# Attention and feed-forward layer on one core: the softmax sums' reciprocals taken on one row per head, by way of DRAM

## The chip, the cores and the metric

One Trainium2 chip, one core of it. The metric is the device time of one execution in microseconds (us), as the median of several runs.

## What is computed

```python
x  = L0_attn_x                                  # (2, 1024, 512), fp32
Q  = (x @ Wq.T + bq)  ->  32 heads of 16;  K, V: 8 heads of 16, each used by 4 query heads
Q, K = rope(Q, K)
w  = softmax(Q @ K.T / sqrt(16))                # per batch and head, 1024 x 1024
x  = layernorm(x + (w @ V) @ Wo.T + bo)
h  = silu((x @ gate_w.T) * gate_s) * ((x @ up_w.T) * up_s)     # 1408 wide
x  = layernorm(x + (h @ down_w.T) * down_s)
```

## The kernel before, in words

**Units, quarters, turns.** The attention is cut into 32 units (`UNITS`, line 37): batch, half of the sequence (512 queries), and one of the 8 K/V heads `g` with its 4 query heads. Eight units of one batch and half make a quarter (0 to 3). Each unit has 8 steps of 128 keys. The main loop (line 684) takes two steps at a time; this document calls one pass of it a *turn*, c = 0 to 127. Unit u has turns 4u to 4u+3 for its exponentials.

**Inside a turn** TensorE follows an order written out by hand (lines 669 to 676): `F`, one piece of other work (fill); `A`, products of Q and K for the row maxima, 12 steps ahead (`max_pass`, line 326), each read by a VectorE maximum (line 342); `B`, the same products again with the maximum subtracted (`exp_pass`, line 363), read by a ScalarE exponential (line 379); and the slots `V0` and `V1`, where the weights of two steps before are multiplied with V (`av`, line 383). Stretches between two turns are measured from V0 to V0. The PSUM banks that hold what TensorE has made and the others have not read are few: four for A and fill, three for B.

**The sums.** The V operand `va` holds a one beside each of its columns (line 137), so a unit's result `pv` has 128 rows: for each of 4 heads 16 pairs of a numerator and the sum of the weights. All 16 sum rows of a head are the same. V1 of turn 4u+4 ends unit u and calls `unit_out` (line 400): ScalarE copies `pv` to `o` (line 406), and SP moves the even rows into `num` and the odd rows into `den` (lines 413 and 414), two transfers of 64 rows of 2 KB. Two units with an even and the next odd g share one `num` and one `den` of 128 rows: a pair. After the odd one, VectorE takes the reciprocal of `den` in four pieces of 128x128 (line 419) and multiplies `num` by it (line 424). There are 16 pairs, the last two units' pair among them.

**When.** Work that is to wait goes by `after(n, f)` (line 192), run in the V slot n steps later (two steps are one turn). `early` (line 189) runs at the start of a given turn, ahead of its F. Before the change a pair's reciprocals stand at the start of turns c+2 and c+3 and the product at c+4, where c is the turn in which the pair's second unit ended; at the end of a quarter (g = 7) the reciprocals stand at the next V0 and V1 and the product at the V0 after these, because three turns after the quarter's end its projection (`project`, line 470) reads `num`.

**Fill.** In turns 0 to 20 it is the projections to Q, K and V (`qk_block`, line 236). VectorE and ScalarE also round 33 pieces of the feed-forward weights in turns 2 to 18 (`piece_round`, line 167), two a turn, and SP stores the rounded pieces (`wsd<-sr`) and loads those of two turns later (`sw`). From turn 35 on the fill is the projection and feed-forward of the quarter before (`quarter`, line 609). Turns in between, and those at a quarter's end, have none.

**SP.** All transfers are issued by SP, in the order of the program, and an instruction that waits holds up all behind it: Q and K stores (`qT`, `kT`), weight pieces, `num` and `den`, the maxima through DRAM (`md`, `mt` in `max_rows`, line 344), the loads of a unit's Q and K (`KS`, `QH`, `QL` in `prep`, line 311), weights (`wt`, `wd_sb`), residual rows (`xq`, `xs`) and results. `max_rows` runs at the end of turns 4k+1, one of them right behind every unit's end.

Of the kernel before, what the change touches and what calls it, by code (L numbers as in the profile page):

```python
# [7 lines left out]
F32 = mybir.dt.float32  # L8
# [3 lines left out]
ALU = mybir.AluOpType  # L12
# [4 lines left out]
P = 128  # L17
B, T, D = 2, 1024, 512
HQ, HKV, HD = 32, 8, 16
G = HQ // HKV  # L20
E = 32
# [7 lines left out]
HALF = 512  # L29
NH = T // HALF  # L30
# [16 lines left out]
def attn_ffn_kernel(tc, x, wqkv, bqkv, wo, bo, rope, wg, wu, wd, gs, us, ds, out):  # L47
    nc = tc.nc

    def pool(name, bufs=1, **kw):  # L50
        return tc.alloc_tile_pool(name=name, bufs=bufs, **kw)
# [3 lines left out]
    dram2 = pool("dram2", 2, space=DRAM)  # L55
    ap1 = pool("ap1")
    ap2 = pool("ap2", 2)
# [96 lines left out]
    def piece_load(i):  # L154
        if i >= PIECES:
            return
        SW[i] = sp4.tile([P, D], F32, tag="sw", name="sw")
        if i < 2 * NF:
            f, up = divmod(i, 2)
            nc.sync.dma_start(  # L160
                out=SW[i].rearrange("p (c n) -> p c n", n=P),
                in_=(wu if up else wg)[:, :, f * P : (f + 1) * P],
            )
        else:
            nc.sync.dma_start(out=SW[i], in_=wd[:, i - 2 * NF, :])

    def piece_round(i):
        w = SW.pop(i)
        SR[i] = sp4.tile([P, D], F32R, tag="sr", name="sr")
        nc.scalar.copy(SR[i], w)  # L170

        nc.vector.scalar_tensor_tensor(
            low, w.bitcast(I32), LOW, low, ALU.bitwise_and, ALU.bitwise_or
        )

    def piece_store(i):
        nc.sync.dma_start(out=wsd[i], in_=SR.pop(i).bitcast(F32))
# [8 lines left out]
        after(4, lambda: nc.vector.tensor_reduce(flag, flr, AX.X, ALU.max))  # L186

    later = {}
    early = {}
    now = [0]  # L190

    def after(n, f):
        later.setdefault(now[0] + n, []).append(f)
# [132 lines left out]
    def max_pass(n, j, i):  # L326
        u, s = divmod(n, US)
        t, half = divmod(s, NH)
        if u not in MX:
            MX[u] = ap2.tile([P, TH, G, NH], F32, tag="mx", name="mx")  # L330
        r = slice(j * E, (j + 1) * E)
        if i == 0:
            PA[n, j] = ps_a[0].tile([P, HALF], F32, tag="pa", name="pa")
        nc.tensor.matmul(  # L334
            PA[n, j],
            (QH, QL)[i][u][r, t * P : (t + 1) * P],
            KS[u][r, half * HALF : (half + 1) * HALF],
            start=i == 0,
            stop=i == 1,
        )  # L340
        if i == 1:
            nc.vector.tensor_reduce(MX[u][:, t, j, half : half + 1], PA.pop((n, j)), AX.X, ALU.max)  # L342
# [36 lines left out]
            nc.scalar.activation(prob[:, j, :], PB.pop((n, j)), AF.Exp, scale=SCALE)  # L379

    PV, PVN, NUM = {}, {}, {}

    def av(n, prob):
        u, kc = divmod(n, US)
        b, qh, g = UNITS[u]
        done = PVN[u] = PVN.get(u, -1) + 1
        if done == 0:
            PV[u] = ps_v.tile([P, HALF], F32, tag="pv", name="pv")
        for j in range(G):
            nc.tensor.matmul(  # L390
                PV[u][j * E : (j + 1) * E, :],
                vas[b][:, kc, g, :, :].rearrange("p d o -> p (d o)"),
                prob[:, j, :],
                start=done == 0,
                stop=done == US - 1,
            )
        if done == US - 1:
            unit_out(u)

    def unit_out(u):  # L400


        b, qh, g = UNITS[u]
        q = u // HKV
        o = ap1.tile([P, HALF], F32, tag="o", name="o")
        nc.scalar.copy(o, PV.pop(u))  # L406
        if g % 2 == 0:
            NUM[q, g // 2] = ap4.tile([P, HALF], F32, tag="num", name="num")
            NUM["den"] = ap1.tile([P, HALF], F32, tag="den", name="den")
        num, den = NUM[q, g // 2], NUM["den"]  # L410
        r0 = (g % 2) * G * HD
        rows = slice(r0, r0 + G * HD)
        nc.sync.dma_start(out=num[rows, :], in_=o[0:P:2, :])
        nc.sync.dma_start(out=den[rows, :], in_=o[1:P:2, :])
        if g % 2:
            c = now[0] // 2
            for k in range(TH):
                ns = slice(k * P, (k + 1) * P)
                f = lambda ns=ns: nc.vector.reciprocal(den[:, ns], den[:, ns])  # L419
                if g == HKV - 1:  # L420
                    after(k // 2 + 1, f)
                else:
                    early.setdefault(c + 2 + k // 2, []).append(f)
            f = lambda: nc.vector.tensor_tensor(num, num, den, ALU.mult)
            if g == HKV - 1:
                after(3, f)
            else:
                early.setdefault(c + 4, []).append(f)


    XQ, FP = {}, {}
    DONE = set()
    LASTQ = B * NH - 1

    def load_residual(q, t):
        b, qh = divmod(q, NH)
# [33 lines left out]
    def project(q, t):  # L470
        py = bank("py")
        for c in range(NC):
# [6 lines left out]
            )  # L479
        if q == LASTQ:  # L480
            row = XQ[q, t]
# [26 lines left out]
    def hidden(q, f, up):  # L508
# [13 lines left out]
        if not up:  # L522
# [15 lines left out]
        pus = FP["tmp"].tile(  # L538
            [P, HALF], F32, tag="pus" if q == LASTQ else "th", name="pus"
        )  # L540
        nc.scalar.mul(pus, p, ust[:, f : f + 1])  # L541

        def rest():
            nc.gpsimd.tensor_tensor(z, pus, z, ALU.mult)  # L544
            if q == LASTQ:
                nc.scalar.copy(hi, z)
# [7 lines left out]
    def down(q, t, f0=0, f1=NF):  # L554
# [14 lines left out]
        ys = fp1.tile([P, D], F32, tag="ys", name="ys")  # L569
        if q == LASTQ:  # L570
            nc.vector.tensor_tensor(ys, pd, dsb, ALU.mult)
# [8 lines left out]
        def store():  # L580
# [4 lines left out]
            for i in range(TH):  # L585
                if (q + 1, i) not in XQ and q < LASTQ and (q + 1, i) not in DONE:
                    if i <= t + (q + 1 == LASTQ):
                        DONE.add((q + 1, i))
# [89 lines left out]
    def v_hook(n):  # L678
        now[0] = n
        for f in later.pop(n, ()):  # L680
            f()

    before = None
    for c in range(STEPS // 2):
        probs = {}

        pieces = [i for i in (2 * c - 4, 2 * c - 3) if 0 <= i < PIECES]
        for i in pieces:
            piece_round(i)
        if pieces:  # L690
            after(1, lambda ps=pieces: [(piece_store(i), piece_load(i + 4)) for i in ps])
        for f in early.pop(c, ()):
            f()
        alone = 2 * c + LEAD >= STEPS
        has_fill = bool(fill) and fill[0][0] <= c
        if c >= (STEPS - QS) // 2:
            has_fill = has_fill and len(fill) > 2
        for s in NO_A if alone else WITH_FILL if has_fill else NO_FILL:
            if s == "F":
                if has_fill:  # L700
                    fill.pop(0)[1]()

                    while c < (STEPS - QS) // 2 and (rest := len(fill) % PHASES) and QS // 2 - 1 - c % (QS // 2) < rest < DOWNS:
                        fill.pop(0)[1]()
                continue
            n = 2 * c + int(s[-1])
            if s[0] == "V":
                v_hook(n)
                if before is not None:
                    av(n - 2, before[n - 2])  # L710
                continue
            j, i = int(s[1]), "abc".index(s[2])
            if s[0] == "A":
                max_pass(n + LEAD, j, i)
                continue
            if i == 2 and n not in probs:
                probs[n] = ap3.tile([P, G, HALF], F32, tag="prob", name="prob")
            exp_pass(n, j, i, probs.get(n), alone)
        before = probs
        u, s = divmod(2 * c + 1, US)  # L720
        if s == US - 1 and u + 3 < len(UNITS):
            prep(u + 3)
        if (2 * c + 1 + LEAD) % US == US - 1 and not alone:
            max_rows((2 * c + 1 + LEAD) // US)
        if c == QS // 2 - 10:
            low_flag()
        if c == QS // 2 - 6:
            sp4.release()
            qp4.release()
            qp2.release()  # L730
            qp1.release()
            fp1 = pool("fp1", side="right")
            fp2 = pool("fp2", 2, side="right")
            fp5 = pool("fp5", 5, side="right")
            wd_sb = fp1.tile([P, NF, D], F32R, name="wd_sb")
            nc.sync.dma_start(
                out=wd_sb.bitcast(F32), in_=wsd[2 * NF : PIECES].rearrange("f p n -> p f n")
            )
            FP["tmp"] = fp1
            ask_weights(RING - 1)  # L740
            for t in range(TH):
                load_residual(0, t)
            for q in range(B * NH - 1):
                fill.extend(quarter(q))
# [15 lines left out]
    n = 2 * STEPS  # L760
# [137 lines left out]
```

## Time and profile before

| | |
|---|---|
| runs of the kernel | 1229.11, 1231.25, 1236.65 us, median 1231.25 |
| profiled execution | 1231.15 us |
| its span, first to last instruction | 1229.3 us |
| mean granted TensorE clock | 0.973 of full speed |
| busy: TensorE / VectorE / ScalarE / GpSimd | 1174.0 / 875.3 / 704.4 / 353.2 us |
| transfers by SP | 125.30 MB, 32.0% of the 16 engines' span |

Lines of the profile: `L342 DVE TENSOR_REDUCE mx<-pa 128x1 f32<-128x512 f32` is line 342 of the kernel on VectorE, writing tile mx from tile pa. PE is TensorE, PEld its weight loads, DVE VectorE, ACT ScalarE, POOL GpSimd, SPq the queue of SP. The windows view gives, for a stretch of time, its length, then the busy time of each engine with the number of its instructions, the granted TensorE clock, the busy share of the DMA engines and GB/s. In a timeline a row starts with its start and length in us; in brackets stands the idle time before it and what ended it. In the view of waits, the three numbers are us in total, times, and the longest one.

### The profile page before, as it was taken

How to read it: one execution, taken by the hardware profiler on the slowest of the kernel's cores; microseconds unless marked ns; L12 is line 12 of the kernel's file. 1: busy time of each engine (PE TensorE's matmuls, PEld its weight loads, DVE VectorE, ACT ScalarE, POOL GpSimd, SP SyncE). 2: the span in 40 equal slices, each digit the busy share in tenths (PEclk: the TensorE clock that was granted, in tenths of full speed). 3: DMA queues.
4: the chain of work that ended last, by engine and by line, in shares of the span. 5: the costliest groups of instructions: out<-in, count | busy, mean ns of one | idle time of the engine just before them, and what ended most of it. 6: DMA issues, size and time to landing. Idle time of an engine off the chain costs nothing.

```text
span 1229.3 us, 22709 instructions
## 1 busy us (share of the span) xinstructions
PE 1174.0 (96%) x8784; PEld 611.6 (50%) x8784; DVE 875.3 (71%) x1492; ACT 704.4 (57%) x1300; POOL 353.2 (29%) x340
## 2 busy tenths in 40 slices
PE   8799999999999999999999999999899999999996
PEld 5354445444444544545544544556444454554585
DVE  3579898878877787876677878784758878732434
ACT  2016767656655677675445777774536776774251
POOL 3127262540103122223522222225412222225431
PEclk9769999999989999999999999999999999999899
DMA  5357777442612222221212222221312222111230
GB/s 161 103 190 241 257 243 253 147 162 55 206 45 61 80 79 79 80 82 67 88 33 82 79 79 79 79 79 56 110 36 94 82 79 79 50 49 53 94 121 37
DMA packets 82291, 126.80 MB, mean 103 GB/s; under 512 B 15873, under 2 KB 29442, under 8 KB 82050
## 3 DMA queue, kind: packets, MB, share of 16 engines
q1 hardware_dynamic: 82178, 125.30, 32.0%
q8 instruction: 71, 1.16, 0.4%
q14 instruction: 42, 0.34, 0.1%
HBM read 80.43 MB, written 36.44 MB: 95 GB/s over the span
## 4 chain that ended last, share of the span: by engine, by line
PE 73%; DVE 17%; DMA 3%; POOL 3%; issue 2%; ACT 1%; SPq 0%; POOLq 0%; DVEq 0%; ACTq 0%
PE pb L371 16%; PE pv L390 16%; PE pg L514 13%; PE pa L334 12%; DVE mx L342 9%; PE pq L242 5%; PE pd L560 5%; PE py L473 4%; DVE den L419 3%; DVE st L458 1%; POOL xq L577 1%; POOL ys L576 1%; ACT prob L379 1%; DMA fl<-red 1%; PE pv L293 1%
## 5 line engine op out<-in xcount | busy, mean ns | idle before, releaser
L342 DVE TENSOR_REDUCE mx<-pa 128x1 f32<-128x512 f32 x1024 | 644.5, 682 | 183.7 <-PE pa L334 179.6
L379 ACT ACTIVATE prob<-pb 128x512 f32<-128x512 f32 x1024 | 545.7, 599 | 268.9 <-PE pb L371 253.5
L334 PE MATMUL pa<-KS,QH 32*128 32x512 f32 x1024 | 364.9, 469 | 33.6 <-DVE mx L342 15.0
L334 PE MATMUL pa<-KS,QL 32*128 32x512 f32 x1024 | 350.5, 433 | 0.1
L371 PE MATMUL pb<-QH,KS 32*128 32x512 f32 x1024 | 318.1, 475 | 1.0 <-ACT prob L379 1.0
L390 PE MATMUL pv<-prob,va 128*32 128x512 f32 x2048 | 277.1, 613 | 0.0
L371 PE MATMUL pb<-QL,KS 32*128 32x512 f32 x1024 | 273.5, 421 | 0.0
L371 PE MATMUL pb<-mt,ones 32*128 32x512 f32 x1024 | 256.7, 397 | 0.0
L334 PEld LDWEIGHTS pa<-KS,QH 32*128 32x128 f32 x1024 | 152.8, 187 | 157.9 <-DVE mx L342 131.9
L544 POOL TENSOR_TENSOR z<-pus,z 128x512 f32<-128x512 f32 x44 | 56.3, 1279 | 449.8 <-ACT pus L541 422.6
L371 PEld LDWEIGHTS pb<-QH,KS 32*128 32x128 f32 x1024 | 134.3, 183 | 83.1 <-issue 50.5
L371 PEld LDWEIGHTS pb<-QL,KS 32*128 32x128 f32 x1024 | 127.6, 184 | 86.1 <-issue 85.5
L334 PEld LDWEIGHTS pa<-KS,QL 32*128 32x128 f32 x1024 | 162.9, 189 | 5.7 <-DMA QL<-qT 0.9
L371 PEld LDWEIGHTS pb<-mt,ones 32*128 32x128 f32 x1024 | 140.4, 185 | 25.3 <-issue 17.3
L514 PE MATMUL pg<-x1h,wt 128*128 128x512 f32 x352 | 146.3, 416 | 0.7 <-ACT x1h L503 0.7
L514 PE MATMUL pg<-x1l,wt 128*128 128x512 f32 x352 | 139.4, 396 | 0.3 <-DVE x1l L504 0.3
L390 PEld LDWEIGHTS pv<-prob,va 128*32 128x32 f32 x2048 | 40.9, 108 | 94.5 <-issue 83.3
L514 PEld LDWEIGHTS pg<-x1h,wt 128*128 128x128 f32 x352 | 67.0, 190 | 38.1 <-issue 22.7
L242 PE MATMUL pq<-xT,wqkv_sb 128*128 128x512 f32 x160 | 77.7, 632 | 0.0
L514 PEld LDWEIGHTS pg<-x1l,wt 128*128 128x128 f32 x352 | 67.1, 191 | 13.1 <-DVE x1l L504 0.8
L560 PE MATMUL pd<-wd_sb,hh 128*128 128x512 f32 x176 | 69.9, 397 | 0.7 <-ACT o L406 0.7
L560 PE MATMUL pd<-wd_sb,hl 128*128 128x512 f32 x176 | 68.6, 390 | 0.0
(80 smaller groups left out, 978.5 us busy)
## 6 DMA issues: line engine op xcount, KB each, us to landing
wt<-wsd SPq DMA_DIRECT2D x88, 256.0 KB
KS<-kT SPq DMA_DIRECT2D x128, 128.0 KB
wsd<-sr SPq DMA_DIRECT2D x33, 256.0 KB
qT<-hi SPq DMA_DIRECT2D x16, 512.0 KB
qT<-lo SPq DMA_DIRECT2D x16, 512.0 KB
QH<-qT SPq DMA_DIRECT2D x32, 256.0 KB
QL<-qT SPq DMA_DIRECT2D x32, 256.0 KB
xs<-in_x_dram SPq DMA_DIRECT2D x16, 256.0 KB
```

The lines of the kernel that those rows point to most:

```text
L242: nc.tensor.matmul(pq, wqkv_sb[:, c, m * P : (m + 1) * P], XT[b, half][:, c, :], start=c == 0, stop=c == NC - 1,)
L293: nc.tensor.matmul(pv[:, t, :], XT[b, half][:, c, t * P : (t + 1) * P], wqkv_sb[:, c, KV:W], start=c == 0, stop=c == NC - 1,)
L334: nc.tensor.matmul(PA[n, j], (QH, QL)[i][u][r, t * P : (t + 1) * P], KS[u][r, half * HALF : (half + 1) * HALF], start=i == 0, stop=i == 1,)
L342: nc.vector.tensor_reduce(MX[u][:, t, j, half : half + 1], PA.pop((n, j)), AX.X, ALU.max)
L371: nc.tensor.matmul(PB[n, j], ones[r, :] if i == 2 else KS[u][r, kc * P : (kc + 1) * P], (QH[u], QL[u], mts[u % 2])[i][r, :], start=i == 0, ...
L379: nc.scalar.activation(prob[:, j, :], PB.pop((n, j)), AF.Exp, scale=SCALE)
L390: nc.tensor.matmul(PV[u][j * E : (j + 1) * E, :], vas[b][:, kc, g, :, :].rearrange("p d o -> p (d o)"), prob[:, j, :], start=done == 0, st ...
L419: f = lambda ns=ns: nc.vector.reciprocal(den[:, ns], den[:, ns])
L473: nc.tensor.matmul(py, NUM[q, c][:, t * P : (t + 1) * P], wo_sb[:, c, :], start=c == 0, stop=c == NC - 1,)
L514: nc.tensor.matmul(p, w[:, c, :], x1[:, c, :], start=c == 0 and k == 0, stop=c == NC - 1 and k == 1,)
L544: nc.gpsimd.tensor_tensor(z, pus, z, ALU.mult)
L560: nc.tensor.matmul(pd, h[:, f, t * P : (t + 1) * P], wd_sb[:, f, :], start=f == 0 and k == 0, stop=f == NF - 1 and k == 1,)
```

## The change

For all pairs but the last of the last quarter (30 of the 32 units): only one of the 16 equal sum rows of each of the unit's 4 heads is stored to DRAM (`sd`, 4 rows of 512), read back as 128 rows of 16 (`rc`), inverted there by one reciprocal of 128x16, stored to DRAM (`rd`), and read back four times, each row to the 16 rows of its head in `den`. The inverse stands at the V slot two steps after the unit's end (V1 of the next turn), for each unit, and the product four steps after the pair's second unit (V1 of the turn after that one). `early` is gone. The last pair keeps its four pieces in the slots that g = 7 had.

```diff
-    early = {}
...
         nc.sync.dma_start(out=num[rows, :], in_=o[0:P:2, :])
+        if q < LASTQ or g // 2 < HKV // 2 - 1:
+            sd = dram2.tile([G, HALF], F32, tag="sd", name="sd")
+            rd = dram2.tile([G, HALF], F32, tag="rd", name="rd")
+            rc = ap2.tile([P, G * HALF // P], F32, tag="rc", name="rc")
+            nc.sync.dma_start(out=sd, in_=o[1:P:E, :])
+            nc.sync.dma_start(out=rc, in_=sd.rearrange("j (p n) -> (j p) n", n=G * HALF // P))
+
+            def inverse():
+                nc.vector.reciprocal(rc, rc)
+                nc.sync.dma_start(out=rd.rearrange("j (p n) -> (j p) n", n=G * HALF // P), in_=rc)
+                for j in range(G):
+                    nc.sync.dma_start(
+                        out=den[r0 + j * HD : r0 + (j + 1) * HD, :],
+                        in_=rd[j : j + 1, :].to_broadcast([HD, HALF]),
+                    )
+
+            after(2, inverse)
+            if g % 2:
+                after(4, lambda: nc.vector.tensor_tensor(num, num, den, ALU.mult))
+            return
         nc.sync.dma_start(out=den[rows, :], in_=o[1:P:2, :])
         if g % 2:
-            c = now[0] // 2
             for k in range(TH):
                 ns = slice(k * P, (k + 1) * P)
-                f = lambda ns=ns: nc.vector.reciprocal(den[:, ns], den[:, ns])
-                if g == HKV - 1:
-                    after(k // 2 + 1, f)
-                else:
-                    early.setdefault(c + 2 + k // 2, []).append(f)
-            f = lambda: nc.vector.tensor_tensor(num, num, den, ALU.mult)
-            if g == HKV - 1:
-                after(3, f)
-            else:
-                early.setdefault(c + 4, []).append(f)
+                after(
+                    k // 2 + 1, lambda ns=ns: nc.vector.reciprocal(den[:, ns], den[:, ns])
+                )
+            after(3, lambda: nc.vector.tensor_tensor(num, num, den, ALU.mult))
...
-        for f in early.pop(c, ()):
-            f()
```

More of the change, by code (lines that the diff above doesn't have):

```diff
@@ L381, in attn_ffn_kernel @@
     PV, PVN, NUM = {}, {}, {}
+    LASTQ = B * NH - 1
     def av(n, prob):
@@ L413, in unit_out @@
         nc.sync.dma_start(out=num[rows, :], in_=o[0:P:2, :])
+        if q < LASTQ or g // 2 < HKV // 2 - 1:
[16 more added lines that the diff above has]
+            return
         nc.sync.dma_start(out=den[rows, :], in_=o[1:P:2, :])
         if g % 2:
-            c = now[0] // 2
             for k in range(TH):
                 ns = slice(k * P, (k + 1) * P)
-                f = lambda ns=ns: nc.vector.reciprocal(den[:, ns], den[:, ns])
-                if g == HKV - 1:
-                    after(k // 2 + 1, f)
-                else:
-                    early.setdefault(c + 2 + k // 2, []).append(f)
-            f = lambda: nc.vector.tensor_tensor(num, num, den, ALU.mult)
-            if g == HKV - 1:
-                after(3, f)
-            else:
-                early.setdefault(c + 4, []).append(f)
+                after(
+                    k // 2 + 1, lambda ns=ns: nc.vector.reciprocal(den[:, ns], den[:, ns])
+                )
+            after(3, lambda: nc.vector.tensor_tensor(num, num, den, ALU.mult))
     XQ, FP = {}, {}
     DONE = set()
-    LASTQ = B * NH - 1
     def load_residual(q, t):
```

## The prediction

> **What bounds the kernel now.** I read the page's chain first, then the windows view from V slot to V slot (a turn), then the issue times of SP.
>
> ```profile
> PE 73%; DVE 17%; DMA 3%; POOL 3%; issue 2%; ACT 1%; SPq 0%; POOLq 0%; DVEq 0%; ACTq 0%
> ```
>
> The groups by line (busy us, mean ns, idle before):
>
> ```profile
> L419 DVE RECIPROCAL den<-den 128x128 f32<-128x128 f32 x64 | 55.6, 913 | 12.4 <-DMA den<-o 12.4
> ...
> L424 DVE TENSOR_TENSOR num<-num,den 128x512 f32<-128x512 f32 x16 | 12.5, 782 | 0.0
> ```
>
> TensorE sets the time nearly everywhere. The reciprocals are 55.6 us of VectorE work, and 2.6% of the chain is theirs (about 32 us), but the chain names whoever worked last, not what would be saved. That is read from turns with and without reciprocals. Columns: length of the turn, then busy time of PE, PEld, DVE, ACT and POOL, the granted clock, DMA.
>
> ```profile
> 428.54:436.38 7.84, 7.75 (x68) 3.83 (x65) 7.47 (x13) 5.08 (x10) 3.14 (x3) 1.00 0.23 71
> 458.65:465.92 7.27, 7.27 (x68) 3.78 (x64) 5.09 (x9) 4.97 (x10) 3.15 (x3) 1.00 0.24 78
> 265.90:272.20 6.30, 6.16 (x63) 2.83 (x64) 5.38 (x9) 3.69 (x8) 0.00 (x0) 1.00 0.34 126
> 346.45:355.00 8.55, 7.22 (x58) 3.46 (x57) 8.41 (x17) 4.48 (x9) 0.00 (x0) 0.93 0.01 2
> 355.00:370.44 15.44, 15.44 (x73) 6.13 (x72) 6.82 (x12) 4.11 (x8) 0.00 (x0) 0.82 0.02 2
> 370.44:383.30 12.86, 12.61 (x77) 5.26 (x73) 7.69 (x15) 4.24 (x8) 5.76 (x6) 1.00 0.29 83
> ```
>
> The first two rows are the same kind of turn, once with three reciprocals and once with none: 0.57 us apart, though the three cost 2.7 us of VectorE. The rest was idle VectorE. The last four are about a quarter's end: turn 33 holds four reciprocals and takes 8.55 us, where a turn of its kind takes 6.3; the turn after it runs at a clock of 0.82.
>
> **What is removed.** (1) Eight pairs inside the last three quarters: six at 0.57, two at 0.56 and 0.92 (turns 106 and 114): 4.9 us. (2) Three quarter ends. The end at 346: 8.55 + 15.44 against 6.3 + 12.8 gives 4.9 us. The 12.8 is the 12.86 row, confirmed by the other ends with their clock loss taken off. The ends at 616 (9.28 + 13.73) and 884 (7.99 + 14.47) give 3.9 and 3.4. Together 12.2 us. (3) Turns 26 and 27 (7.86 and 6.98 us, without fill) against 6.2 and 6.1: 2.5. (4) Turns 10, 11 and 18: 0.8, 0.4 and 0.1 over 8.87: 1.3. The pair at turn 122 runs where VectorE is idle: nothing. Sum: **20.9 us**. VectorE as a whole is relieved of 60 x 0.9 = 54 us, of which 33 lay under TensorE.
>
> About half of (2) is the clock:
>
> ```profile
> 351.11 0.39 PE L371 MATMUL pb<-mt,ones 32*128 32x512 f32 x1
> 352.73 1.08 PE L334 MATMUL pa<-KS,QH 32*128 32x512 f32 x2 [1.23 <-DVE mx L342]
> ```
>
> TensorE stood for 1.23 us here, and in the trace's clock record the grant is 0.5 for the 6.8 us after 353.7. The stalls of 1.72 and 1.25 us at the other ends are followed by 3.4 us at 0.5 each: 6.8 us lost in all. The Trainium skill ("TensorE: Matmul & The Clock Gate", Why this matters for your kernels) allows idle gaps up to about 3 us. By that rule these dips would not belong to the reciprocals, would stay, and (2) would be 5.4 us instead of 12.2. I take the row, since a dip follows each of the three stalls within 3 us; but three cases are few, and the rule stays in the range.
>
> **What is added on VectorE.** Thirty reciprocals of 128x16. Nearest rows: a 128x128 reciprocal 896 ns, a 128x16 reduction 186. I take 0.2 us each (0.11 by the element count alone to 0.9 if all of it were fixed). They fall into gaps of 0.3 us between the maxima in steady turns: nothing. Without the gap, 30 x 0.2 = 6 us.
>
> **What is added on SP and in transfers.** Per unit, `den<-o` goes; sd, rc, rd and four den transfers come: six issues more, 180 in all on a queue in strict order, with three waits for landings (rc for sd, den for rd, rd for VectorE). Landing times are the completions in the trace, from issue: num 2.8 us, a 4x2 KB load (mt) 1.88, a 32x128 B store (md) 1.43. One row is far off: the flag's 128 stores of 4 bytes.
>
> ```profile
> SPq L360 <- DMA md<-mr: 31.7, 44, 2.3
> SPq L185 <- DMA fl<-red: 7.5, 1, 7.5
> ```
>
> rd stores 128 rows of 64 B. The Trainium skill ("DMA: Bandwidth & Descriptors", Specifications) puts every transfer under 512 B down as a read-modify-write, which speaks for the flag's price, 7.9 us. But md is under 512 B as well and lands in 1.43. 64 B is nearer to 128 than to 4, so I take 1.43. By the rule rd would be 6.4 us later at each unit: a rival below. rc I take as mt, 1.9.
>
> Steady unit: num issue at T; sd lands at T+2.9, rc at T+4.9. VectorE reaches the inverse at T+6.9 (417.66 and 424.6), so no wait. Then 0.2 + 1.5 (rd) + 4 x 0.58 (issues) + 1.3 (rest of the last landing) = 5.3 us, while the product stands one turn later, 7.4: spare 2 us. Behind the product wait the maxima, and behind them TensorE. At a quarter end the turn is 6.2 us, the spare 0.9. md and mt move back by 1 to 2 us and are wanted two turns later: nothing.
>
> **Where it does not hold: the first half.** Up to turn 16 SP pauses only for mr, once per unit, and num lands in 5 us.
>
> ```profile
> 123.77 0.69 SPq L413 DMA_DIRECT2D num<-o  x1
> 124.52 0.59 SPq L414 DMA_DIRECT2D den<-o  x1
> ...
> 130.38 0.60 SPq L160 DMA_DIRECT2D sw<-in_wu_dram  x1
> 134.53 1.72 SPq L357 DMA_DIRECT2D md<-mr  x4
> 137.32 1.12 SPq L360 DMA_DIRECT2D mt<-md  x2
> ```
>
> Unit 0: rc waits for sd until 129.0; the six transfers behind it (qT, wsd, sw) go out by 134.4 instead of 131.0; rd lands behind them at about 139; den until 141.3; then md, mt until 145.7, against 138.4 now. The sw pieces behind land 7 us later, at 157 instead of 150.0, and VectorE waits for that piece already now (150.12). ScalarE and VectorE stand, TensorE loses about 5 us and 1.7 of clock: **6.7** (2 to 9). Unit 1: den lands 2.6 us after the product's place at 173.5: 2.3 and half a dip, **3.2** (0 to 5). Unit 2: **0.7** (0 to 3). Unit 5 (turn 25): sd behind KS loads lands at 296, rc at 298.2, VectorE is there at 297.0: **0.5** (0 to 2).
>
> Unit 6 (turn 29): its num is held back by the loads of wd_sb, wt and xq.
>
> ```profile
> 308.62 8.59 SPq L439 DMA_DIRECT2D xq<-in_x_dram  x4
> 317.61 2.28 SPq L317 DMA_DIRECT2D KS<-kT  x4
> ...
> 323.01 0.52 SPq L413 DMA_DIRECT2D num<-o  x1
> ```
>
> Now nobody minds, since the pair's reciprocals come 24 us later. After the change: num lands at 327.7, rc at 329.8, and 1.8 us more since unit 5's den transfers push wd_sb back; VectorE arrives at 322, two us earlier than now. It stands for 9 us, TensorE for 8, and a dip of 1.7 follows: **9.7** (4 to 13). Sum of the new waits: **20.8** (6 to 32).
>
> **Sum.** 1229.3 - 20.9 + 20.8 = 1229.2 us of span; the profiled execution took 1231.15 with its surroundings, and the median of the runs is 1231.25, so 2 us more: 1231.
>
> **Rivals.**
> *The waits are mostly covered (0.2).* While SP stands, the engines of the DMA drain, and what follows lands sooner (3.2 to 4.7 us after the pause at 102 instead of 5.3). With the low ends, 6 us: 1216. Against it: unit 6's delay is bandwidth, and nothing hides it.
> *SP becomes the bound of the first half (0.2).* Each unit adds some 11 us to SP (4 for sd, 0.9 for two issues, 4.2 for rd behind the others, 1.7 net for den), and SP's only pauses are the waits for mr, 3.5 to 4.9 us per unit. If lateness is carried on from unit to unit instead of being reset by each stall, four units lose 6 us each where I have 10.6 for all: with the high end at unit 6, 1247, slower than before. It decides once more than about 5 us per unit are not covered.
> *rd at the flag's price (0.1).* 6.4 us late against 2 of spare: 4 us at each of eight products, 5.5 at three ends, a dip of up to 1.7 at each, and more at the first units: about 1298. It decides from a landing of 3.4 us on.
> That the change does not do what it says can be left out: the 60 large reciprocals are gone from the program.
>
> **How the numbers follow.** Forecast 0.5, rivals 0.2, 0.2, 0.1. Its own range is 1231 - 15 = 1216 to 1231 + 12 = 1243, from the ends of the new waits. To leave out no more than 2 in 10 the range goes from 1214 to 1256. One per cent, 12 us, is about what can be told from no change. Faster is the first rival: 0.2. Slower are the others: 0.3. Same: 0.5.
>
> **What would show it.** Right: turns 42, 50, 58 at 7.27; turn 33 at 6.3 and 34 at 12.8, no dip at 353, 623 and 893; VectorE idle before the inverse of turn 29 by some 9 us; a wait for sw at turn 8 of about 7. Wrong: rd landing far from 1.43, products waiting in steady turns, dips that stay, or SP keeping its times near 137.

## The result and the profile after

| | before | after |
|---|---|---|
| median of the runs | 1232.64 us (20 runs, 1227.40 to 1236.65, and one of 1757.50) | 1227.09 us (20 runs, 1223.19 to 1231.02) |
| ratio | | 0.9953, 95% interval 0.9942 to 0.9964 |
| profiled execution: span, mean clock | 1229.3 us, 0.973 | 1226.4 us, 0.970 |
| VectorE / TensorE busy | 875.3 / 1174.0 us | 832.4 / 1171.1 us |

Half a per cent faster: 43 us less work on VectorE, 5.5 us less time by the medians (2.9 us between the two profiled executions). The page of after, the chain's shares by engine:

```profile
PE 76%; DVE 10%; DMA 5%; POOL 4%; issue 2%; ACT 1%; SPq 0%; POOLq 0%; DVEq 0%; ACTq 0%
```

VectorE's share of the chain fell from 17% to 10%, and that of the transfers rose from 3% to 5%. Where the time went is read from the turns. The windows view of after, with turns 8, 10, 29, 33, 34 and 42 (length, busy PE, PEld, DVE, ACT, POOL, granted clock, DMA share, GB/s):

```profile
152.17:167.64 15.47, 11.93 (x69) 4.89 (x66) 8.39 (x15) 8.35 (x15) 5.70 (x5) 0.78 0.95 274
176.51:185.38 8.87, 8.87 (x68) 3.86 (x65) 8.25 (x14) 5.94 (x11) 6.07 (x5) 1.00 0.22 77
327.55:340.05 12.50, 8.10 (x58) 3.92 (x57) 5.80 (x15) 4.46 (x9) 5.01 (x4) 0.86 0.59 154
359.51:365.48 5.97, 5.97 (x58) 3.08 (x57) 5.05 (x12) 4.29 (x9) 0.00 (x0) 1.00 0.08 12
365.48:378.72 13.24, 13.24 (x74) 5.73 (x72) 7.05 (x14) 4.28 (x8) 0.00 (x0) 1.00 0.04 9
436.80:444.06 7.26, 7.26 (x68) 3.80 (x65) 5.60 (x10) 4.97 (x10) 3.14 (x3) 1.00 0.20 49
```

Turn 42 is now as short as a turn without reciprocals (7.26 for 7.84). The quarter's end, turns 33 and 34, takes 5.97 and 13.24 where it took 8.55 and 15.44, at full clock. But turn 8 has grown from 8.87 to 15.47, and turn 29 from 7.36 to 12.50. Before, these two were:

```profile
152.19:161.06 8.87, 8.87 (x69) 3.84 (x65) 7.81 (x13) 6.46 (x12) 5.73 (x5) 1.00 1.07 287
321.13:328.49 7.36, 6.80 (x57) 3.31 (x57) 5.75 (x13) 4.29 (x9) 4.37 (x4) 1.00 0.63 156
```

At turn 8 it is the weight pieces (`sw`) that all wait for (timelines of after: two rows of VectorE, one of ScalarE, one of TensorE; `ACT q` is ScalarE's copy out of a PSUM bank, and stands behind ScalarE's rounding of the piece):

```profile
152.96 0.69 DVE L172 SCALAR_TENSOR_TENSOR low<-sw,low 128x512 int32<-128x512 int32 x1 [4.11 <-DMA sw<-in_wg_dram]
155.96 0.69 DVE L172 SCALAR_TENSOR_TENSOR low<-sw,low 128x512 int32<-128x512 int32 x1 [2.31 <-DMA sw<-in_wu_dram]
```

```profile
155.94 0.62 ACT L170 CAST sr<-sw 128x512 fp32r<-128x512 f32 x1 [2.38 <-DMA sw<-in_wu_dram]
```

```profile
157.20 0.79 PE L333 MATMUL pa<-KS,QH 32*128 32x512 f32 x1 [3.54 <-ACT q L256]
```

All turns that differ from before, in us and added up by place. A dip is a stretch in which the granted clock is halved. no_recip is an experiment below, the kernel before with the 60 reciprocals left out and nothing added:

| place | predicted | after | no_recip |
|---|---|---|---|
| eight pairs inside quarters 1 to 3 | -4.9 | -4.7 | -4.8 |
| three quarters' ends | -12.2 | -11.6 | -11.9 |
| turns 26, 27 | -2.5 | -2.6 | -2.6 |
| turns 10, 11, 18 | -1.3 | -1.3 | -1.3 |
| turn 8 (unit 0) | +6.7 | +6.6 | 0 |
| turn 10 (unit 1's den) | +3.2 | 0 | - |
| turns 13, 14, 16 (unit 2) | +0.7 | +1.9 | 0 |
| turns 24, 25 (unit 5) | +0.5 | +2.0 | +1.8 |
| turns 29, 30 (unit 6) | +9.7 | +6.7 | +6.1 |
| turns 95, 96 (a dip) | 0 | +1.5 | 0 |
| sum | -0.1 | -1.5 | -12.7 |

The tile view of after for `rc`, and the times from issue to landing, answer the costs that the prediction bounded:

```profile
L420 SPq DMA_DIRECT2D rc<-sd x30: 320/320/328, 128.0 to 1075.2; - x30
L423 DVE RECIPROCAL rc<-rc x30: 241/243/253, 130.9 to 1079.4; 128x16 f32<-128x16 f32 x30
L424 SPq DMA_DIRECT2D rd<-rc x30: 319/320/687, 134.0 to 1079.7; - x30
...
who waited for it (us, times):
  DVE rc L423: 7.9, 2
```

An inverse of 128x16 takes 0.243 us (0.2 taken). From issue to landing the medians, worked out from the completions in the trace, are 2.16 us for sd, 1.65 for rc, 1.40 for rd and 1.81 for den. VectorE waited for rc at two units of 30, 7.9 us together, and of 15 products one waited for den, 1.7 us.

### The profile page after: what moved, and what is told of

It is laid out like the page before. It is cut to its first block, busy times and chain, and to the rows that moved or that the text cites. A ratio compares the mean times of both kernels' runs of the same rounds, so it can differ in the third digit from the quotient of the medians.

```text
span 1226.4 us, 22934 instructions
## 1 busy us (share of the span) xinstructions
PE 1171.1 (95%) x8784; PEld 612.2 (50%) x8784; DVE 832.4 (68%) x1462; ACT 703.3 (57%) x1300; POOL 353.4 (29%) x340
## 4 chain that ended last, share of the span: by engine, by line
PE 76%; DVE 10%; DMA 5%; POOL 4%; issue 2%; ACT 1%; SPq 0%; POOLq 0%; DVEq 0%; ACTq 0%
PE pb L370 17%; PE pv L390 17%; PE pg L527 14%; PE pa L333 13%; PE pq L241 5%; DVE mx L341 5%; PE pd L573 4%; PE py L486 3%; DVE st L471 1%; POOL xq L590 1%; POOL ys L589 1%; DMA xq<-in_x_dram 1%; DMA wt<-wsd 1%; POOL xq L481 1%; DMA fl<-red 1%
## 5 line engine op out<-in xcount | busy, mean ns | idle before, releaser
L370 PE MATMUL pb<-QH,KS 32*128 32x512 f32 x1024 | 321.4, 478 | 1.0 <-ACT prob L378 1.0
```

The source lines that it names most:

```text
L370: nc.tensor.matmul(PB[n, j], ones[r, :] if i == 2 else KS[u][r, kc * P : (kc + 1) * P], (QH[u], QL[u], mts[u % 2])[i][r, :], start=i == 0, ...
```

## The experiments

Theory after these views: the removed part is right, and it is eaten in the first quarter, by SP standing for landings (turn 8) and by a wait at turn 29. Rival: six transfers more cost every unit a little. The kernels of one group ran on one chip beside the same runs of before; across groups only the ratios compare. There are 4 to 19 runs of each kernel. "Loop" is the time from V0 of turn 1 to V0 of turn 127 in one profiled execution, against that of before, in us (after: -1.7).

| group | kernel | us | ratio to before, 95% | loop |
|---|---|---|---|---|
| 1 | q0_only | 1242.27 | 1.0043 (1.0024 to 1.0062) | +12.7 |
| 1 | from_q1 | 1218.14 | 0.9862 (0.9836 to 0.9888) | -11.0 |
| 1 | no_recip | 1216.62 | 0.9853 (0.9826 to 0.9879) | -13.2 |
| 1 | one_a_slot | 1224.81 | 0.9918 (0.9889 to 0.9946) | -4.2 |
| 2 | after_again | 1223.48 | 0.9947 (0.9929 to 0.9965) | -5.4 |
| 2 | spread_issue | 1220.26 | 0.9935 (0.9912 to 0.9958) | -8.8 |
| 2 | late_loads | 1225.60 | 0.9956 (0.9938 to 0.9974) | -4.1 |
| 2 | q1_slots_late | 1222.79 | 0.9932 (0.9918 to 0.9947) | -5.2 |
| 3 | wd_late | 1219.37 | 0.9891 (0.9867 to 0.9915) | -5.7 |
| 3 | spread_wd | 1212.30 | 0.9857 (0.9836 to 0.9878) | -17.7 |
| 3 | before_wd | 1228.97 | 0.9998 (0.9981 to 1.0016) | +1.4 |
| 4 | spread_best | 1209.49 | 0.9784 (0.9755 to 0.9814) | -19.8 |

Before had medians of 1235.38, 1231.00, 1228.60 and 1237.17 us in the four groups.

after_again is the changed kernel once more. Its loop is nearly 4 us shorter than after's: turn 8 (+6.8), turns 29 and 30 (+7.9) and all that is removed come again, while turns 95 and 96 cost nothing, turns 24 and 25 only 0.2 and turns 13 to 16 0.6. So the table's losses of 2 us and less vary from one execution to the next, and the two large ones do not.

### Where the change pays: q0_only, from_q1

```diff
-        if q < LASTQ or g // 2 < HKV // 2 - 1:
+        if u < HKV:
```

That is q0_only; from_q1 has `HKV <= u < len(UNITS) - 2` there. All other units take the path of before, with `early` and its slots.

> The row by way of DRAM for the eight units of quarter 0 alone; all other pairs as before. Theory (the first quarter pays, the rest gains): the trace of after stood 6.8 us behind that of before at turn 64, so slower than before by about 7 us, 1239 to 1240. Rival (every unit pays a little for six transfers more, and the gain is spread as well): 8 of 30 units would have 8/30 of the whole change, 1.5 us faster than before, about 1231.

> The row by way of DRAM for units 8 to 29 alone; quarter 0 as before. Theory: all that follows turn 64 gained 8.5 us in the loop (12.2 in my sum, of which a new dip at 879 took 1.7): 10 us faster than before, 1222 to 1223, and 4 to 5 faster than after. Rival (the gain is spread): 22/30 of the whole change, 4 us faster than before, 1228 to 1229.

The first quarter alone is slower than before, and the rest alone is 1.4% faster: the rival, which had q0_only faster, falls. from_q1 gained more than expected (17 us by the medians, 11 by the traces). The two ratios together make 0.990 and not after's 0.995; the intervals take up a part of that, the rest stays open.

### What is removed, alone: no_recip

```diff
-                if g == HKV - 1:
+                if u == len(UNITS) - 1:
                     after(k // 2 + 1, f)
-                else:
+                elif False:
                     early.setdefault(c + 2 + k // 2, []).append(f)
```

> The kernel before without the 60 large reciprocals of all pairs but the last; everything else as before, so the numerators are multiplied by the sums and not by their inverses. It leaves out what the change removes and adds nothing. My sum of what is removed says 20.9 us: 1211 to 1212. By the rule of the Trainium skill ("TensorE: Matmul & The Clock Gate") the three dips at the quarters' ends would not belong to the reciprocals and would stay: 14.1 us, 1218 to 1219.

18.8 us less by the medians, between the two expectations (14.1 and 20.9); the loop, 13.2 us less, lies below both. The table shows why: each removal came as summed, 20.6 us, the three dips at the ends with it, and 6.1 us were lost again in turns 29 and 30 and 1.8 in turns 24 and 25, where this kernel adds nothing. The timeline of TensorE in no_recip (start, length; in brackets the idle time before it and what ended it):

```profile
327.58 1.19 PE L334 MATMUL pa<-KS,QH 32*128 32x512 f32 x3 [4.16 <-DMA QH<-qT]
```

And TensorE and VectorE in after at the same place, two timelines:

```profile
335.56 0.47 PE L333 MATMUL pa<-KS,QH 32*128 32x512 f32 x1 [2.98 <-DMA QH<-qT]
337.45 1.38 PE L333 MATMUL pa<-KS,QH 32*128 32x512 f32 x2 [1.42 <-DVE mx L341]
```

```profile
329.09 1.29 DVE L341 TENSOR_REDUCE mx<-pa 128x1 f32<-128x512 f32 x2 [0.34 <-PE pa L333]
336.60 0.25 DVE L423 RECIPROCAL rc<-rc 128x16 f32<-128x16 f32 x1 [6.22 <-DMA rc<-sd]
```

TensorE first waits for the next unit's Q, which was issued behind wd_sb, wt and xq, and only then, for 1.42 us, for a maximum that stands behind VectorE's wait for rc. TensorE started again when Q landed, at 335.56, with VectorE still standing, so what held it for 2.98 us was Q. But only one of the four banks was free: three products of A stood unread since VectorE's last maximum, and after one more TensorE stood again. Had Q been there, it would have stood for the maximum from about 333 to 337.45 (an estimate from these rows, with rc as late as here). The two waits lie over each other, and no_recip shows that Q's alone is enough for the loss.

In before, the reciprocals of turns 26 and 27 let TensorE come later to the same load. Counted from the start of turn 26, and with the completions in the traces, Q has landed at 26.4 us in before and at 26.1 in after, but turn 29 starts at 20.9 in before and at 18.2 in after.

### The loads in front of Q: late_loads, wd_late, before_wd

```diff
+        if c == QS // 2 + 2:
+            nc.sync.dma_start(out=wd_sb.bitcast(F32), in_=wsd[2 * NF : PIECES].rearrange("f p n -> p f n"))
         if c == QS // 2 - 6:
...
-            nc.sync.dma_start(out=wd_sb.bitcast(F32), in_=wsd[2 * NF : PIECES].rearrange("f p n -> p f n"))
```

That is wd_late (from the end of turn 26 to that of turn 34), and before_wd is the same edit on the kernel before; late_loads moves the loads of wt and xq as well, all to `QS // 2 - 3`, turn 29.

> The changed kernel with the loads of wd_sb, wt and the first xq moved from the end of turn 26 to the end of turn 29; nothing else. Theory (at turn 29 TensorE stands because QH and QL lie behind these 5 MB; without the added transfers it stood there as well, 4.2 us, as soon as the reciprocals of turns 26 and 27 were gone): turns 29 and 30 lose most of their 6.6 us, 5 to 6.5 faster than after, about 1221. Rival (my prediction's step: VectorE's wait for unit 6's rc, which the added transfers bring): rc is no longer held back either, so the time alone says the same; but then no_recip would not have had the loss. Rival 2 (the weights are late at turn 39, or md and mt behind them): no gain, 1227 or more.

late_loads missed: turns 29 and 30 are as short as they can be (1.1 us below before), and turn 33 is 7.3 us longer than in after. The timeline of TensorE in late_loads:

```profile
356.51 0.76 PE L333 MATMUL pa<-KS,QH 32*128 32x512 f32 x1 [3.38 <-DMA QH<-qT]
358.71 1.38 PE L333 MATMUL pa<-KS,QH 32*128 32x512 f32 x2 [1.43 <-DVE mx L341]
```

The same two waits, one unit later: the loads stand in front of the next Q there. Moving the whole burst only moved the wait.

> The changed kernel with the load of wd_sb alone moved from the end of turn 26 to the end of turn 34 (it is read from turn 61 on); wt and xq stay. late_loads moved the wait to turn 33, where the next unit's QH came behind the same bytes; here 2.9 of the 5.2 MB go where no Q and K load follows for a turn. Theory (unit 6's loss is the bandwidth that wd_sb takes from QH and from unit 6's num): turns 29 and 30 lose their 6.6 us and turn 33 stays at 5.97: 5 to 7 us faster than after. Rival (the rc of unit 6 is late through SP's own waits): turn 29 keeps 3 us or more.

> The kernel before with the same move of wd_sb and nothing else, as a control for the two above. There TensorE comes late to turn 29 anyway, since turns 26 and 27 hold reciprocals, and waits about a microsecond; theory: 1 to 3 us faster than before. Rival (the move is worth as much by itself, and the gain of the other two is not the change's): 5 us or more.

The windows view of wd_late, turns 29 and 30:

```profile
325.04:331.82 6.78, 6.66 (x57) 3.13 (x56) 4.96 (x12) 4.26 (x9) 0.00 (x0) 1.00 0.04 7
331.82:338.06 6.24, 6.24 (x57) 3.05 (x56) 5.71 (x11) 4.33 (x9) 0.00 (x0) 1.00 0.10 28
```

VectorE's timeline in wd_late, at the inverse of unit 6:

```profile
329.25 0.25 DVE L423 RECIPROCAL rc<-rc 128x16 f32<-128x16 f32 x1 [1.37 <-DMA rc<-sd]
```

Turn 29 falls from 12.50 to 6.78 us, VectorE's wait for rc from 6.22 to 1.37, turn 33 stays at 5.96, and the ratio goes from after's 0.995 to 0.989, 6.9 us, with intervals that don't meet. (The loop shows less, since this execution had two dips of 3 us, told of at the end; the medians, 9.2 us below before for after's 5.5 and 7.5, show less as well.) In the kernel before the same move gives 0.9998 (0.9981 to 1.0016): nothing that can be told, at most 2.3 us of the 1 to 3 expected, and far from the rival's 5. Its turns 29 and 30 are 1.1 us shorter. So the wait for Q is a bound that lay behind the reciprocals of turns 26 and 27, and came out when they left. wd_late moved rc forward with Q, so it doesn't part the two waits; its rival, that rc is late through SP's own waits, falls.

### SP standing for landings: spread_issue

```diff
-            nc.sync.dma_start(out=rc, in_=sd.rearrange("j (p n) -> (j p) n", n=G * HALF // P))
...
-            after(2, inverse)
+            if end:
+                read()
+            else:
+                after(1, read)
+            after(2 if end else 3, inverse)
+            after(2 if end else 5, back)
             if g % 2:
-                after(4, lambda: nc.vector.tensor_tensor(num, num, den, ALU.mult))
+                after(4 if end else 7, lambda: nc.vector.tensor_tensor(num, num, den, ALU.mult))
```

Here `end` is g == 7, `read` the load of rc, and `back` the four den transfers, cut out of `inverse`.

> The changed kernel with the same transfers and inverses, but each issued a slot or more after what it waits for: rc one V slot after sd, the inverse and rd two slots later, den another two, the product another two (at the quarters' ends all as after). SP then has no landing to wait for. Theory (turn 8's 6.6 us come from SP standing for sd and rd while the sw pieces queue behind): the sw pieces go out some 6 us earlier, turn 8 within 2 us of before's 8.87, 4 to 6 us faster than after, about 1222. Rival (the six more issues and the bytes do it, not the waits): turn 8 still 4 us or more above before, and 1226 to 1228.

SP's queue in after, then in spread_issue (timelines; the spans differ by 1.6 us here):

```profile
124.25 0.56 SPq L419 DMA_DIRECT2D sd<-o  x1
128.00 0.32 SPq L420 DMA_DIRECT2D rc<-sd  x1
...
133.97 0.69 SPq L424 DMA_DIRECT2D rd<-rc  x1
137.92 1.71 SPq L426 DMA_DIRECT2D den<-rd  x4
139.73 1.77 SPq L356 DMA_DIRECT2D md<-mr  x4
...
150.44 0.60 SPq L160 DMA_DIRECT2D sw<-in_wu_dram  x1
```

```profile
122.95 0.56 SPq L419 DMA_DIRECT2D sd<-o  x1
123.60 0.56 SPq L274 DMA_DIRECT2D qT<-hi  x1
...
132.95 1.71 SPq L356 DMA_DIRECT2D md<-mr  x4
...
143.06 0.60 SPq L160 DMA_DIRECT2D sw<-in_wu_dram  x1
```

In after SP issues nothing for 3.2 us behind sd and 3.3 us behind rd. In spread_issue other issues stand in these holes, md goes out 6.8 us earlier on the trace's clock, 5.2 with the spans aligned, and the piece that VectorE waits for 7.4 (5.8). Turns 8 and 28 in the windows view of spread_issue:

```profile
150.57:159.43 8.86, 8.86 (x68) 3.86 (x64) 7.79 (x13) 6.44 (x12) 5.72 (x5) 1.00 0.94 274
308.58:325.75 17.17, 7.90 (x59) 3.78 (x57) 6.20 (x11) 4.95 (x10) 5.41 (x4) 0.71 0.78 270
```

The loss at turn 8 is gone to the last hundredth, with the same transfers and bytes: it was the waiting, not their number. The second row shows what the edit broke: turn 28 takes 11 us more, since unit 5's den transfers now stand behind wd_sb, wt and xq. The timeline of VectorE there:

```profile
320.53 0.77 DVE L443 TENSOR_TENSOR num<-num,den 128x512 f32<-128x512 f32 x1 [10.67 <-DMA den<-rd]
```

The ratio therefore moved by a tenth of a per cent only, from after_again's 0.9947 to 0.9935 (the intervals overlap), short of the 4 to 6 us expected, and the verdict rests on turn 8 alone.

### The ends without any transfer: one_a_slot

```diff
                 if g == HKV - 1:
-                    after(k // 2 + 1, f)
+                    after(k + 1 if q < LASTQ else k // 2 + 1, f)
...
-                after(3, f)
+                after(4 if q < LASTQ else 3, f)
```

> The kernel before with the four pieces at the three quarters' ends one to a V slot, in the next four slots, and the product in the fourth; before they are two to a slot in two slots. The same work on VectorE, nothing on SP. Theory (what is lost at the ends is the piling up: VectorE has no room in turn 33, so TensorE stands over a microsecond and the clock halves): most of the 12.2 us come back, 8 to 10 us faster than before, 1223 to 1225. Rival (it is the amount of work, or the clock dips there for another reason): within 3 us of before, 1230 to 1233.

The windows view of one_a_slot, turns 33 and 34:

```profile
348.90:355.27 6.37, 6.27 (x57) 3.13 (x56) 6.26 (x13) 4.27 (x9) 0.00 (x0) 1.00 0.00 0
355.27:368.52 13.25, 13.25 (x72) 5.77 (x71) 8.82 (x16) 4.32 (x8) 0.00 (x0) 1.00 0.02 4
```

Turn 33 holds two reciprocals instead of four and turn 34 the other two: 6.37 and 13.25 us, against 5.97 and 13.24 in after. The three ends gave 4.4, 3.4 and 2.9 us, 10.6 of the 12.2 summed, with all the reciprocals kept. Its loop shows 6 us less, for a dip at turns 29 and 30 and one at 63 and 64; by the medians the kernel is 10.6 us faster.

### The whole: q1_slots_late, spread_wd, spread_best

> Quarter 0 on the path of before, the row by way of DRAM from unit 8 on (1218.1 us so far), and besides: the four pieces at quarter 0's end one to a V slot (4.4 us in the trace of that edit), and the weight loads at the end of turn 29. If the gains add: 1211 to 1214, faster than every kernel so far. If the loads' new place only moves the wait, or the dips come elsewhere: 1215 to 1218.

q1_slots_late (from_q1, one_a_slot's edit at the end of quarter 0, and late_loads' edit) missed: its ratio is 0.993, where 1211 to 1214 us would have been 0.980 to 0.983 beside the same before as from_q1's 1218, and from_q1 alone had 0.986. Turn 33 is 8.2 us longer than in before, since num and den of unit 7 stand behind the late loads. The timeline of VectorE:

```profile
354.40 0.95 DVE L441 RECIPROCAL den<-den 128x128 f32<-128x128 f32 x1 [9.38 <-DMA den<-o]
```

> The issues spread as in spread_issue, unit 5 with its den transfers and product two slots earlier than there (so that they stand ahead of the wt and xq loads), and the load of wd_sb at the end of turn 34. If the three causes are separate, turn 8 costs nothing, the 11 us that spread_issue lost at turn 28 are gone, and turn 29 does not wait: spread_issue's 8.8 us in the loop become 19 to 21, 0.983 to 0.985 of before, about 1211. If a wait for rc or den is left at unit 5 or 6: 1215 to 1220.

> spread_wd with unit 5's inverse one slot earlier and its rd and den transfers right behind it, ahead of md and mt and of the weight loads. In spread_wd the product of that pair waited 3.0 us for den at turn 27, and a dip followed: turns 27 and 28 were 3.1 us longer. If the den transfers land before the product, these 3.1 us go, less up to 1 us where VectorE waits for rc at turn 25: 0.983 to 0.984 of before, about 2 us better than spread_wd. If not: as spread_wd, 0.986.

spread_wd is spread_issue with wd_late's move and an exception for unit 5; spread_best changes that exception:

```diff
-            after(2 if end else 3, inverse)
-            after(2 if end else 3 if u == 5 else 5, back)
+            soon = end or u == 5
+            after(2 if soon else 3, inverse)
+            after(2 if soon else 5, back)
```

spread_wd's loop was 1 to 3 us short of its expectation, and the wait for den at turn 27 (3.0 us) is what was left. In spread_best it is gone there. Its windows view, turns 8, 27, 29, 30, 33 and 34:

```profile
152.49:161.35 8.86, 8.86 (x68) 3.85 (x64) 7.78 (x13) 6.44 (x12) 5.74 (x5) 1.00 0.93 261
307.74:313.69 5.95, 5.95 (x58) 3.05 (x57) 5.56 (x10) 4.34 (x9) 0.00 (x0) 1.00 0.97 314
319.73:325.69 5.96, 5.96 (x58) 3.07 (x58) 4.88 (x10) 4.29 (x9) 0.00 (x0) 1.00 0.04 9
325.68:331.93 6.25, 6.25 (x58) 3.05 (x56) 5.82 (x12) 4.35 (x9) 0.00 (x0) 1.00 0.05 8
343.93:349.88 5.95, 5.95 (x57) 3.06 (x56) 5.02 (x12) 4.28 (x9) 0.00 (x0) 1.00 0.07 8
349.88:363.12 13.24, 13.24 (x73) 5.75 (x71) 7.06 (x14) 4.30 (x8) 0.00 (x0) 1.00 0.52 168
```

TensorE is busy to the end of every one of them, at full clock. The loop is 2.0 us shorter than spread_wd's, as expected; the ratio, 0.9784 (0.9755 to 0.9814), is better than expected, against a before of 1237 us at mean clocks of 0.964 to 0.971, lower than the 0.973 of the profiled one, so that the loop is the safer measure. With 1209.5 us it is the fastest kernel here, and its loop of -19.8 us is about the whole of what was summed as removed. Whether the large reciprocals, spread everywhere as one_a_slot spreads them at the ends, would come as far without any round trip was not tried.

## Why the prediction came out as it did

The forecast of 1231 (no change to be told) lies 4 us above the median, and most single terms hold. But that the total came out is in part luck: two errors of opposite sign nearly cancel. What leaving the reciprocals out is worth in the turns is 12.7 us (no_recip) and not 20.9, since 7.9 are lost again at once; what the transfers cost on top of that is 11.2 us (12.7 less after's 1.5; by the loops of no_recip and after_again 7.8) and not 20.8. Point by point:

- **Removed, 20.9: held place by place.** 20.2 in after and 20.6 in no_recip. Eight pairs 4.7 for 4.9, ends 11.6 for 12.2, turns 26 and 27 2.6 for 2.5, turns 10, 11 and 18 as worked out.
- **The clock at the ends: the row was right, the rule was not.** The dips at 353, 623 and 893 are gone in after, in no_recip and (all reciprocals kept) in one_a_slot. The idle gaps of up to about 3 us that the Trainium skill allows ("TensorE: Matmul & The Clock Gate", Why this matters for your kernels) did not cover stalls of 1.23, 1.72 and 1.25 us.
- **Added on VectorE, nothing: held.** 30 inverses of 0.243 us, and the steady turns are at 7.26.
- **rd at 1.43 and not 7.9: held.** 1.40 in the median. The rule for transfers under 512 B in the Trainium skill ("DMA: Bandwidth & Descriptors", Specifications) cost nothing that can be seen here: rows of 64 B land as fast as md's of 128 B. That rival falls.
- **Turn 8, 6.7: held, mechanism and size** (6.6, of which TensorE stood for 3.5 and lost 3.1 to the clock, for my 5 and 1.7). den went out until 139.6 (141.3 predicted), the last sw piece landed at 155.9 (157).
- **Unit 1, 3.2: failed.** The product did wait for den, 1.7 us for my 2.3, but TensorE had been 100% busy in turn 10 (8.87 of 8.87 us): the wait lay under work that it had, and no dip followed. I counted VectorE's wait as TensorE's.
- **Unit 2, 0.7, and unit 5, 0.5: too small.** 1.9 and 2.0. Unit 5's place has a dip in no_recip too (1.8), so it is hardly the change's.
- **Unit 6, 9.7: the place was right, the account was half.** I had VectorE stand for rc for 9 us and TensorE with it for 8. Measured: 6.2 for rc, and TensorE stood 3.0 us for Q, behind the weight loads, and 1.4 us more for what VectorE owed it. The step that failed is in (3): the 2.5 us of turns 26 and 27 were taken as gained, and I did not ask what TensorE meets when it comes earlier. It meets Q, and no_recip pays 6.1 us for that without any added transfer, where (1) to (4) have nothing. In after the wait for rc lies over the same stretch and adds little, 6.7 in all; so my 9.7 stood in the wrong column, and made up for what I had left out of the other (7.9, with turns 24 and 25). What rc would have cost with Q in time was not measured.
- **The rivals.** "SP bounds the first half" falls as put: the lateness is reset after turn 8 (turns 10 to 12 run as in no_recip). "Mostly covered" is right for unit 1 only.

The medians are kinder than the traces to every kernel but spread_wd (after: 5.5 and 2.9 us). In group 1 the runs of before reach from 1228.3 to 1241.9, and those of no_recip from 1215.9 to 1219.1: executions of before differ by their clock (spans of 1226.4 and 1236.8 us had mean clocks of 0.972 and 0.965), and the profiled one has 0.973.

## What to carry to other kernels

Work taken off an engine that is not the bound is worth what it is worth in each turn, and it brings the next thing that is late: move through the turns after the gain and ask which load TensorE will now reach too early. On a queue in strict order the price of a round trip through DRAM was here not its transfers but what stood behind its waits; issue each leg where its input has landed, and count what stands behind it there as well. Where a burst of work makes the bound engine stand, spreading it over more slots can give most of what removing it gives (10.6 us of 11.6 here).

## What the hardware showed that was not expected

Half clock followed stalls well under 2 us, but not each time. The windows view of after, turns 63, 64, 95 and 96, and of wd_late, turns 63 and 64:

```profile
608.99:616.65 7.66, 6.76 (x61) 2.85 (x57) 6.19 (x11) 4.30 (x9) 7.39 (x7) 1.00 0.14 39
616.66:622.70 6.04, 6.04 (x59) 3.14 (x57) 5.16 (x10) 4.88 (x10) 0.41 (x1) 1.00 0.80 237
871.98:879.92 7.94, 6.74 (x62) 2.89 (x59) 6.47 (x12) 4.47 (x9) 7.67 (x7) 0.96 0.15 46
879.91:887.20 7.29, 7.29 (x57) 3.54 (x57) 4.88 (x9) 4.68 (x10) 1.44 (x2) 0.81 0.58 186
```

```profile
599.46:608.00 8.54, 7.41 (x61) 3.52 (x58) 6.78 (x12) 4.47 (x9) 7.80 (x7) 0.86 0.24 64
608.00:616.10 8.10, 8.10 (x58) 3.40 (x57) 4.68 (x9) 4.75 (x10) 1.27 (x1) 0.72 0.43 147
```

The work in these turns is the same in both kernels. In the first turn of each pair TensorE stands once for longer than about 0.1 us: for 0.62 us (after, turn 63) or 0.90 us (the others). In one execution the clock is then halved for 3.4 or 6.8 us, in another not at all; the longest pair (wd_late, turns 95 and 96) is 3.0 us longer for it. In the 14 traces here these two places come 28 times: a stall of 0.90 us was followed by a dip in 7 cases of 22, one of 0.62 us in none of 4, and one of 1.2 us (spread_wd and spread_best, turn 63) in none of 2. So the length of the stall alone does not decide.

In the traces' clock records all dips of the loops last 3.41 us or 2, 3 or 4 times that (6.83, 10.24 and 13.65). That agrees with the free-running window of about 3.4 us in the Trainium skill ("TensorE: Matmul & The Clock Gate", What's actually happening); but the same section has the clock fall after a whole idle window, and here dips came with only 0.9 us of standing in one piece. Where the stall falls in such a window may decide; that was not tried.
